# Look-ups of a network's weights on GpSimd in a pinned order, gathered rows added a slot after their fetch, weights' loads behind the squares' exchange

## The chip, the cores and the metric

One core of one Trainium2 chip. The metric is device time of one execution in microseconds (us), the median of several runs; lower is better. Engines are named as in the profile: PE (TensorE), PEld (its weight loads), DVE (VectorE), ACT (ScalarE), POOL (GpSimd), SP (SyncE, which here only issues DMAs). "SPq" and "POOLq" are the instruction streams of SP and POOL that issue DMAs. L953 is line 953 of the kernel before the change.

## The reference

Eight sequences of 512 tokens with 256 channels, float32, pass two layers: a rotating scan with gates, a mixture of 16 experts (2 chosen a token), causal attention, and a gated FFN whose weights are looked up in a table of 16 values.

```python
x = x + _L0_attn_ref(_layernorm(x), ...)       # scan over the tokens, 6 heads
x = x + _L0_ffn_ref(_layernorm(x), ...)        # 16 experts, the best 2 of each token
# _L1_attn_ref: 16 heads of 128, causal, 512 tokens
scores = jnp.einsum('biph,biqh->biqp', k, q)
attn = jax.nn.softmax(masked / jnp.sqrt(jnp.float32(d_head)), axis=-1)
z = jnp.einsum('biqp,biph->biqh', attn, v)
out = jnp.einsum('df,bqf->bqd', W_O, z_flat)
# _L1_ffn_ref: 256 -> 688 -> 256
w = lut[idx]                                   # gate, up and down weights
h = jax.nn.silu(gate) * up
```

The change touches the second layer's attention stage, in which three things run beside the attention itself: the results of the experts are gathered and added to x, the FFN's weights are made from indices and table, and the attention's weights are loaded again for each sequence.

## The kernel before, in words

**Stages.** Layer 0 with its router runs until some 390 us, the experts' blocks to some 530, the attention of layer 1 from there to 2046, and the last FFN to the end at 2277. The attention's loop (L1304 on) goes over 64 pairs of heads (8 sequences of 8 pairs) and in each over its two heads, e = 0 and 1: 128 turns, called slots here. Four slots (two pairs) make a quarter of a sequence's output.

**One slot.** In order: scores of 128-row tiles 0 and 1 of this head (PE `sc`, then DVE `ms` with the row's least value, L1074, then ACT `pr`, the exponential, L1085); the head before ("front") has its probabilities `slots` turned in blocks of 32 by DVE (L1108) and written to the squares in DRAM by four DMAs of SP (L1111); part of the products for the next pair's queries and keys (`nxt`); the head two before ("rear") is weighed: PE `pz` (L1140) from `pT` and `v`, copied by ACT to `zT` (L1147); pending additions of outputs (`in_time`); a gather; a step of the look-ups; the next group's values (`ahead`); scores of tiles 2 and 3; then `exchanged` (L1113), in which SP loads `pT` back from the squares, turned as a whole. There is one `pT` buffer.

**Products of seven.** Queries, keys, values and outputs are made by seven products in place of eight (class Sevens, L230). `first` gives four of them into banks pa and pb, and DVE (sometimes ACT for the copy) makes `p`, `u`, `p` and the first quarter of the result (L249 to L253). `second` gives three more into the same banks, so PE waits for L253 before it goes on with pb, and DVE adds u to it (L262).

**Weights.** `following_weights` (L1001) is called where a weights' tile has been used for the last time; it issues at once two or three loads by SP (L739 to L745), which wait until PE is done with the buffer. Queries' and keys' weights have two buffers each, values' ("v") and outputs' ("o") one. In the first sequence `complete_weights` makes the sums that the products need on POOL (L201 to L205) and writes them to DRAM by a DMA of POOL (L747); later sequences load them.

**Look-ups.** `lookups` (L933) is a generator that does a step each time it is called: in every slot of the sequences 1 to 7, so 112 times. A part of the indices is loaded by ACT's queue (L944); for each of the 16 values DVE compares the indices with it and multiplies by the table's entry (L947, L950), and adds the product to the sum (L953). Four parts of 128 x 688 (`fs`, one value a step) and six of up to 128 x 256 (`fd`, two values a step). Behind the fourth part come four copies (L960) and five sums of fs, one a step.

**Gathers.** `gather` (L890) fetches 128 rows of experts' results by an indirect DMA that POOL issues (L893, buffer `yg`, two of them) and adds them to x by DVE (L900), in the same slot. The rows of sequences 1 to 7 are spread over the first 88 slots: 56 gathers.

**Outputs.** A quarter's `combined` (L1166) makes four differences of 128 x 512 on POOL (`zS`, one buffer), then four pieces of products with the "o" weights follow in later slots, and after a sequence's last quarter `summed` (L1207) makes eight sums on POOL and two pieces of transposes on PE (L1229) read them. `one_out` starts the next piece, at one or two places of a slot.

**What sets the order.** In the loop, the order of PE, DVE and SP is that of the program (manual_schedule, L1287); that of ACT and POOL is made by the scheduler of the language. Each engine runs its own stream in order and waits for semaphores.

Of the kernel before, what the change touches and what calls it, by code (L numbers as in the profile page):

```python
# [10 lines left out]
F32 = mybir.dt.float32  # L11
I32 = mybir.dt.int32
AF = mybir.ActivationFunctionType
ALU = mybir.AluOpType
# [3 lines left out]
P = 128  # L18
NB, T, D = 8, 512, 256
NT = T // P  # L20
# [20 lines left out]
SQ = 32  # L41
# [74 lines left out]
def two_layers(ctx: ExitStack, tc: tile.TileContext, a: dict, out: bass.AP):  # L116
# [79 lines left out]
    def sum_steps(w, eng=nc.vector):  # L196

        a11, a12, a21, a22 = (w[:, n, :] for n in (W_1, W_2, W_3, W_4))
        s1, s2 = w[:, W_5, :], w[:, W_6, :]
        return [  # L200
            lambda: eng.tensor_tensor(s1, a21, a22, ALU.add),  # L201
            lambda: eng.tensor_tensor(s2, s1, a11, ALU.subtract),
            lambda: eng.tensor_tensor(w[:, W_7, :], a11, a21, ALU.subtract),
            lambda: eng.tensor_tensor(a21, a12, s2, ALU.subtract),
            lambda: eng.tensor_scalar(a22, a22, -1.0, None, ALU.mult),  # L205
        ]
# [680 lines left out]
                if s % 12 == 9 and 0 < s // 12 <= 5 or s % 12 == 1 and 1 < s // 12 <= 6:  # L887
                    complete[s % 12 == 1]()

    def gather(b, pool, t, k):  # L890

        y = pool.tile([P, D], F32, name="yg")
        nc.gpsimd.indirect_dma_start(  # L893
            out=y,
            out_offset=None,
            in_=ys,
            in_offset=bass.IndirectOffsetOnAxis(ap=yrow[:, (b * 2 + k) * NT + t : (b * 2 + k) * NT + t + 1], axis=0),
        )
        xt = x_sb[b][:, t, :]
        nc.vector.scalar_tensor_tensor(xt, y, share[:, b, k, t : t + 1], xt, ALU.mult, ALU.add)  # L900

    ygp = ctx.enter_context(tc.tile_pool(name="yg", bufs=2))
    xnp = ctx.enter_context(tc.tile_pool(name="xn", bufs=4))
    with tc.manual_schedule(engines={ENG.PE}):


        first_xn = []
        stats = {}
        for t in range(NT + 1):
            if t < NT:  # L910
                for k in range(2):
                    gather(0, ygp, t, k)
                stats[t] = tile_stats(0, t)
            if t:
                mean, rs = stats[t - 1]
                nc.vector.reciprocal(rs, rs)
                first_xn.append(normed_row(0, xnp, t - 1, mean, rs))
        for b in BEHIND:
            for piece in seqs[b].shared():
                piece()  # L920
# [12 lines left out]
    def lookups(pool):  # L933

        parts = [
            (fs[:, n, :], a[f"idx{w}"][c * P : (c + 1) * P, :], P)
            for n, w, c in ((W_1, 0, 0), (W_2, 0, 1), (W_4, 1, 1), (W_3, 1, 0))
        ]
        behind = []
        parts += [(fd[:k, i, :], a["idx2"][r : r + k, :], k) for i, (r, k) in enumerate(ICH)]  # L940
        for dst, src, k in parts:
            n = src.shape[1]
            idx = pool.tile([P, INTER], I32, tag="idx", name="idx")
            nc.scalar.dma_start(out=idx[:k, :n], in_=src)  # L944
            for v in range(NLUT):
                if v == 0:
                    nc.vector.tensor_scalar(dst, idx[:k, :n], 0.0, lut[:k, 0:1], ALU.is_equal, ALU.mult)  # L947
                else:
                    tmp = pool.tile([P, INTER], F32, tag="tmp", name="tmp")
                    nc.vector.tensor_scalar(  # L950
                        tmp[:k, :n], idx[:k, :n], float(v), lut[:k, v : v + 1], ALU.is_equal, ALU.mult
                    )
                    nc.vector.tensor_add(dst, dst, tmp[:k, :n])  # L953
                if n > T or v % 2:
                    if behind:
                        behind.pop(0)()
                    yield
            if dst is parts[3][0]:
                for n, c, at in ((W_1, 0, APART), (W_2, 1, APART), (W_4, 1, 0), (W_3, 0, 0)):
                    nc.vector.tensor_copy(over[:, c, at : at + OVER], fs[:, n, NF * P :])  # L960
                behind = sum_steps(fs[:, :, : NF * P])


    xtp = ctx.enter_context(tc.tile_pool(name="xt", bufs=2, side="right"))
    with tc.tile_pool(name="big", bufs=2, side="right") as big, tc.tile_pool(
# [31 lines left out]
            return [pool.tile([P, T], F32, tag=tag, name=tag).rearrange("p (k t) -> p k t", k=2) for _ in range(2)]  # L997

        incomplete = []

        def following_weights(n, part):  # L1001
            if part is not None:
                w, complete = load_weights(n, part, part not in seen_parts[n])
                weights[n].append(w)
                seen_parts[n].add(part)
                if complete:
                    incomplete.append((n, complete))
# [49 lines left out]
        class Head:  # L1057
# [29 lines left out]
            def normalized(self, *tiles):  # L1087

                if 0 in tiles:
                    self.slots = ap2.tile([P, NQ, NS, SQ], F32, name="slots")  # L1090
                w = self.slots
                rd = self.rd[:, tiles[0] : tiles[-1] + 1]
                nc.vector.reciprocal(rd, self.den[:, tiles[0] : tiles[-1] + 1])  # L1093
                for i in tiles:

                    for j in range(0, i + 1, 2):
                        n = min(i + 1 - j, 2)
                        at, step = SLOT[j, i], SLOT[j + n - 1, i] - SLOT[j, i]
                        nc.scalar.activation(  # L1099
                            w[:, :, at : at + step + 1 : max(step, 1), :].rearrange("p q j k -> p j q k"),  # L1100
                            self.pr[i][:, j * P : (j + n) * P].rearrange("p (j q k) -> p j q k", q=NQ, k=SQ),
                            AF.Copy,
                            scale=self.rd[:, i : i + 1],
                        )

            def squares_turned(self):

# [27 lines left out]

            def weigh(self):

                pz = pzp.tile([P, T], F32, tag="pz", name="pz")
                for j in range(NT):
                    nc.tensor.matmul(  # L1140
                        pz[:, j * P :].rearrange("p (i q k) -> p i q k", q=NQ, k=SQ),
                        self.v(j),
                        self.of_keys(j),
                        start=(j == 0),
                        stop=(j == NT - 1),
                    )
                nc.scalar.copy(self.z, pz)  # L1147


        late = []  # L1150
# [1 line left out]
        def in_time():  # L1152
            while late:
                late.pop(0)()
# [82 lines left out]
        def outputs(quarter, eng=nc.gpsimd):  # L1237

            quarter.combined(eng)
            last = quarter.q == NGRP - 1  # L1240
            n = quarter.b * NGRP + quarter.q + 1

            def end(*banks):
                quarter.products(3, *banks)
                if n < NB * NGRP:
                    following_weights("o", n % NGRP)
                if last:
                    in_time()
                    quarter.summed(eng)

            pieces = [lambda *banks, i=i: quarter.products(i, *banks) for i in range(3)] + [end]
            if last:
                pieces += [lambda *banks, h=h: quarter.turned(h, *banks) for h in range(2)]
            return pieces

        def one_out():
            if tiles_out:
                tiles_out.pop(0)()
# [1 line left out]
        ALL = NB * NPAIR  # L1260

        together = {1: (1,), 2: (2, 3), 4: (4, 5), 6: (6, 7), NB: (0,)}
        rows_to_gather, since = [], 0
        for c in (1, 2, 4, 6):
            until = (c - 1) * 2 * NPAIR + 2 * NT
            rows = [(b, ygp, t, k) for b in together[c] for t in range(NT) for k in range(2)]
# [17 lines left out]
            pattern=[[-1, P]],  # L1284
            channel_multiplier=1,
        )
        with tc.manual_schedule(engines={ENG.PE, ENG.DVE, ENG.SP}):  # L1287
            seqs[0].xn = first_xn
            for c in range(NC):
                seqs[0].turned(c)  # L1290
            seqs[0].combined()
            following_weights("o", 0)

            pairs[0].first(0)
            pairs[0].first(1, lambda: other_banks(psc, "sc"))
# [3 lines left out]
            groups[0].first(1, lambda: other_banks(ptp, "pt"))  # L1299
            for s in range(2):  # L1300
                groups[0].second(s, s or None)

            front = rear = None
            for p in range(ALL):  # L1304
# [6 lines left out]
                for e in range(2):  # L1311
# [20 lines left out]
                    if rear:  # L1332
                        rear.weigh()
                    in_time()
                    while rows_to_gather and rows_to_gather[0][0] <= 2 * p + e:
                        gather(*rows_to_gather.pop(0)[1])
                    if b:
                        next(look, None)
                    if rear and e and pair % 2 == 0:
                        quarter = Outputs(*divmod(p // 2 - 1, NGRP), done, kept)  # L1340
                        tiles_out += outputs(quarter)
# [11 lines left out]
                    head.scores(3)  # L1353
                    if front and front.by_slots:
                        front.exchanged()
                    in_time()
                    if e and ahead:
                        last_half = p % 2 == 1
                        ahead.second(p % 2, (p // 2 + 2) % NGRP if last_half and p // 2 + 2 < len(groups) else None)
                    if not e and nxt:  # L1360
                        nxt.first(1)
                    if head.by_slots:
# [1 line left out]
                        head.normalized(3)  # L1364

                    complete_weights(*(("v",), (0, 1, "o"))[e])
                    front, rear = head, front

                    if pair == 3 and e == 0 and b + 1 in together:
# [12 lines left out]
                if pair % 2 == 1:  # L1382
                    done = z
            one_out()
            rear.weigh()
            one_out()
            front.turned()
# [208 lines left out]
```

## Time and profile before

| what | us |
|---|---|
| median of 3 runs | 2278.41 |
| lowest and highest run | 2270.70, 2278.88 |
| the profiled execution, its own time | 2278.94 |
| its span, first to last instruction | 2277.2 |
| busy PE, PEld | 2123.3, 1551.5 |
| busy DVE, ACT, POOL | 1716.0, 1181.6, 428.1 |
| DMA: share of 16 engines' time, mean rate | q1 47.5%, q0 3.4%; 160 GB/s |
| granted TensorE clock, mean | 0.989 |

The page gives busy time by engine, the span in 40 slices, the costliest groups of instructions with the idle time of the engine just before them and what ended it. A table of windows gives the same by stretches of time, a list of waits says which engine waited at which instruction for whom (total us, times, longest), a list by form keeps operand shapes apart (count, total us and mean ns of one), and a timeline shows the instructions in order. PE counts as busy to the modelled end of a matmul; idle time of an engine that isn't the bound costs nothing.

### The profile page before, as it was taken

The page shows a single profiled execution, that of the slowest core. Times are in us where ns is not written, and L with a number is a line of the kernel's source. Part 1 is how long each engine was busy: PE and PEld are TensorE (multiplying, and loading weights), DVE is VectorE, ACT ScalarE, POOL GpSimd, SP SyncE. Part 2 cuts the span into 40 slices and gives each one's busy share as a digit, 9 for nine tenths or more (in the row PEclk, how much of TensorE's full clock was granted, in tenths as well). Part 3 has the DMA queues.
Part 4 walks back from the last instruction along what each step waited for, and adds up shares of the span by engine and source line. Part 5 has one row for each costly group of instructions (what it writes and reads, how often), then busy time and mean ns, then how long its engine had stood idle before and what let it go on. Part 6 is the DMA issues. An engine that isn't in the chain of part 4 may idle for free. (4 is left out here: it accounts for less than half of the span.)

```text
span 2277.2 us, 29531 instructions
## 1 busy us (share of the span) xinstructions
PE 2123.3 (93%) x8733; PEld 1551.5 (68%) x8733; DVE 1716.0 (75%) x4269; ACT 1181.6 (52%) x2943; POOL 428.1 (19%) x438
## 2 busy tenths in 40 slices
PE   6999998998899999999999999988999999989999
PEld 3554545886577776777677777766776767658887
DVE  6788887555667778778777877888877887868765
ACT  5767761433565555555556555545555555643211
POOL 0022234002463312121221131121011111010000
PEclk9999999999999999999999999999999999999999
DMA  5111217652677766666757666765666675530000
GB/s 192 46 70 64 75 63 247 193 159 82 191 223 223 221 200 199 211 204 201 226 186 213 205 210 193 215 199 174 185 191 199 190 213 182 176 94 10 19 19 28
DMA packets 208640, 363.98 MB, mean 160 GB/s; under 512 B 27120, under 2 KB 145952, under 8 KB 208480
## 3 DMA queue, kind: packets, MB, share of 16 engines
q1 hardware_dynamic: 197712, 333.62, 47.5%
q0 software_dynamic: 8112, 25.31, 3.4%
q10 hardware_dynamic: 2656, 3.17, 0.4%
q8 instruction: 70, 1.15, 0.2%
q14 instruction: 90, 0.74, 0.1%
HBM read 241.29 MB, written 120.72 MB: 159 GB/s over the span
## 5 line engine op out<-in xcount | busy, mean ns | idle before, releaser
L1099 ACT ACTIVATE slots<-pr,rd 128x128 f32<-128x128 f32 x756 | 302.2, 463 | 236.2 <-DVE rd L1093 162.1
L1140 PE MATMUL pz<-pT,v 128*128 128x512 f32 (+3 forms) x1024 | 306.8, 443 | 30.1 <-DMA pT<-squares 29.7
L1070 PE MATMUL sc<-qk,qk 128*128 128x128 f32 (+3 forms) x1024 | 321.4, 437 | 4.6 <-DVE low L1074 4.5
L1085 ACT ACTIVATE pr<-ms,low 128x128 f32<-128x128 f32 (+3 forms) x512 | 282.0, 552 | 41.1 <-DVE low L1074 39.5
L1140 PEld LDWEIGHTS pz<-pT,v 128*128 128x128 f32 x1024 | 192.0, 192 | 158.7 <-issue 63.9
L1074 DVE CUSTOM_DVE_ANT_0 ms<-sc,mask 128x128 f32<-128x128 f32 (+3 forms) x512 | 235.8, 482 | 50.4 <-PE sc L1070 46.9
L1108 DVE STREAM_TRANSPOSE slots<-slots 128x1280 f32<-128x1280 f32 x126 | 190.2, 1510 | 102.0 <-ACT slots L1099 101.9
L1147 ACT COPY zT<-pz 128x512 f32<-128x512 f32 x128 | 74.9, 585 | 281.9 <-PE pz L1140 260.4
L239 PE MATMUL pb<-tT,w 128*128 128x256 f32 x762 | 208.8, 383 | 3.6 <-DVE qk L253 3.0
L1070 PEld LDWEIGHTS sc<-qk,qk 128*128 128x128 f32 x1024 | 174.9, 193 | 52.0 <-ACT slots L1099 5.3
L893 POOL DMA_INDIRECT yg<-ys,yrow x64 | 66.1, 1032 | 613.2 <-DVE x L900 452.8
L239 PEld LDWEIGHTS pb<-tT,w 128*128 128x128 f32 x762 | 140.2, 192 | 23.1 <-DVE qk L253 5.9
L239 PE MATMUL pa<-xT,w 128*128 128x256 f32 x508 | 151.6, 380 | 0.0
L239 PE MATMUL pb<-wv,tT 128*128 128x256 f32 x378 | 106.5, 390 | 39.9 <-DVE v L253 31.6
L632 POOL DMA_INDIRECT xs<-xn,slot x64 | 83.8, 1309 | 306.1 <-DVE share L642 122.8
L251 DVE TENSOR_TENSOR u<-pa,p 128x256 f32<-128x256 f32 x230 | 96.3, 419 | 50.3 <-ACT p L249 45.3
L239 PEld LDWEIGHTS pb<-wv,tT 128*128 128x128 f32 x378 | 68.2, 189 | 89.8 <-DVE v L253 65.3
L1194 PE MATMUL po<-zS,wo 128*128 128x256 f32 x512 | 125.9, 379 | 1.2 <-DVE kept L1205 1.2
L252 DVE TENSOR_TENSOR p<-pb,u 128x256 f32<-128x256 f32 x230 | 97.5, 424 | 25.1 <-PE pb L239 1.8
L262 DVE TENSOR_TENSOR qk<-pb,u 128x512 f32<-128x512 f32 x127 | 85.1, 670 | 38.0 <-PE pb L239 35.3
L1171 POOL TENSOR_TENSOR zS<-zT 128x512 f32<-128x512 f32 x31 | 40.4, 1302 | 372.8 <-PE po L1194 372.8
L1194 PEld LDWEIGHTS po<-zS,wo 128*128 128x128 f32 x512 | 97.2, 190 | 15.2 <-issue 2.1
(314 smaller groups left out, 4256.7 us busy)
## 6 DMA issues: line engine op xcount, KB each, us to landing
squares<-slots SPq DMA_DIRECT2D x504, 160.0 KB
pT<-squares SPq DMA_DIRECT2D x126, 640.0 KB
w<-sqk SPq DMA_DIRECT2D x112, 320.0 KB
w<-in_aqk SPq DMA_DIRECT2D x144, 128.0 KB
wv<-sv SPq DMA_DIRECT2D x28, 640.0 KB
wo<-so SPq DMA_DIRECT2D x28, 640.0 KB
xb<-xs SPq DMA_DIRECT2D x79, 128.0 KB
ys<-yb SPq DMA_DIRECT2D x79, 128.0 KB
```

The source lines that it names most:

```text
L239: nc.tensor.matmul(to, lhsT, rhs, start=first, stop=True, skip_group_check=True)
L251: nc.vector.tensor_tensor(self.u2, pa[:, 1, :], p1, ALU.add)
L252: nc.vector.tensor_tensor(p1, pb[:, 0, :], self.u2, ALU.add)
L262: nc.vector.tensor_tensor(self.out[:, :2, :], pb, self.u2.unsqueeze(1).to_broadcast([P, 2, HT]), ALU.add)
L632: nc.gpsimd.indirect_dma_start(out=xs, out_offset=bass.IndirectOffsetOnAxis(ap=slot[:, k, t : t + 1], axis=0), in_=self.xn[t], in_offset=None,
L1070: nc.tensor.matmul(sc[:, :kw], self.qT[:, i * P : kw], self.kT[:, :kw], start=True, stop=True)
L1074: nc.vector.tensor_tensor_reduce(out=ms[:, :kw], in0=sc[:, :kw], in1=mask[:, T - kw :], scale=-1.0 / math.sqrt(DH), scalar=3e38, op0=ALU.a ...
L1085: nc.scalar.activation(pr, ms[:, :kw], AF.Exp, bias=low, scale=-1.0, accum_out=self.den[:, i : i + 1])
L1099: nc.scalar.activation(w[:, :, at : at + step + 1 : max(step, 1), :].rearrange("p q j k -> p j q k"), self.pr[i][:, j * P : (j + n) * P].r ...
L1108: nc.vector.transpose(self.slots, self.slots)
L1140: nc.tensor.matmul(pz[:, j * P :].rearrange("p (i q k) -> p i q k", q=NQ, k=SQ), self.v(j), self.of_keys(j), start=(j == 0), stop=(j == NT ...
L1194: nc.tensor.matmul(po[:, m, :], self.w[:, n, k * P : (k + 1) * P], self.sides[n][:, k, :], start=(k == 0), stop=(k == 1),)
```

## The change

1. In `lookups` every operation goes from DVE to POOL: comparisons, additions, the four copies and the five sums. The index loads are issued by POOL's queue in place of ACT's, each at the end of the part before; the first is issued ahead of the loop. The step is called at the end of a slot (behind `complete_weights`) and not behind the gather.
2. POOL joins the engines whose order in the loop is that of the program.
3. `gather` becomes `fetched`, which issues the fetch and hands back the addition; in the loop the addition is made a slot later, at the same place of the slot, ahead of the next fetch.
4. `following_weights` only notes what is to be loaded, but for "o"; `load_following` issues the noted loads, behind `exchanged` and again behind the values' second products.
5. A sequence's last quarter has an empty piece between its products and its transposes.
6. `weigh` writes `pz` with the slots' order of queries (q, i, k), so that PE reads `pT` in long runs; ACT's copy puts them in order.
7. `normalized` names its operands first; its branch for DVE is never taken.

```diff
-    def gather(b, pool, t, k):
+    def fetched(b, pool, t, k):
...
         xt = x_sb[b][:, t, :]
-        nc.vector.scalar_tensor_tensor(xt, y, share[:, b, k, t : t + 1], xt, ALU.mult, ALU.add)
+        return lambda: nc.vector.scalar_tensor_tensor(xt, y, share[:, b, k, t : t + 1], xt, ALU.mult, ALU.add)
...
-        for dst, src, k in parts:
+
+        def indices(dst, src, k):
+            idx = pool.tile([P, INTER], I32, tag="idx", name="idx")
+            nc.gpsimd.dma_start(out=idx[:k, : src.shape[1]], in_=src)
+            return idx
+
+        idx = indices(*parts[0])
+        yield
+        for m, (dst, src, k) in enumerate(parts):
             n = src.shape[1]
-            idx = pool.tile([P, INTER], I32, tag="idx", name="idx")
-            nc.scalar.dma_start(out=idx[:k, :n], in_=src)
             for v in range(NLUT):
                 if v == 0:
-                    nc.vector.tensor_scalar(dst, idx[:k, :n], 0.0, lut[:k, 0:1], ALU.is_equal, ALU.mult)
+                    nc.gpsimd.tensor_scalar(dst, idx[:k, :n], 0.0, lut[:k, 0:1], ALU.is_equal, ALU.mult)
                 else:
                     tmp = pool.tile([P, INTER], F32, tag="tmp", name="tmp")
-                    nc.vector.tensor_scalar(
+                    nc.gpsimd.tensor_scalar(
                         tmp[:k, :n], idx[:k, :n], float(v), lut[:k, v : v + 1], ALU.is_equal, ALU.mult
                     )
-                    nc.vector.tensor_add(dst, dst, tmp[:k, :n])
+                    nc.gpsimd.tensor_add(dst, dst, tmp[:k, :n])
+                if v == NLUT - 1 and m + 1 < len(parts):
+                    following = indices(*parts[m + 1])
...
-                    nc.vector.tensor_copy(over[:, c, at : at + OVER], fs[:, n, NF * P :])
-                behind = sum_steps(fs[:, :, : NF * P])
+                    nc.gpsimd.tensor_copy(over[:, c, at : at + OVER], fs[:, n, NF * P :])
+                behind = sum_steps(fs[:, :, : NF * P], nc.gpsimd)
+            idx = following
...
         def following_weights(n, part):
             if part is not None:
+                to_load.append((n, part))
+                if n == "o":
+                    load_following()
+
+        def load_following():
+            while to_load:
+                n, part = to_load.pop(0)
                 w, complete = load_weights(n, part, part not in seen_parts[n])
...
-                pz = pzp.tile([P, T], F32, tag="pz", name="pz")
+                pz = pzp.tile([P, NQ, NT, SQ], F32, tag="pz", name="pz")
                 for j in range(NT):
                     nc.tensor.matmul(
-                        pz[:, j * P :].rearrange("p (i q k) -> p i q k", q=NQ, k=SQ),
+                        pz[:, :, j:, :].rearrange("p q i k -> p q (i k)"),
                         self.v(j),
-                        self.of_keys(j),
+                        self.pT[:, :, SLOT[j, j] : SLOT[j, j] + NT - j, :].rearrange("p q i k -> p q (i k)"),
...
-                nc.scalar.copy(self.z, pz)
+                nc.scalar.copy(self.z.rearrange("p (i q k) -> p i q k", q=NQ, k=SQ), pz.rearrange("p q i k -> p i q k"))
...
             if last:
-                pieces += [lambda *banks, h=h: quarter.turned(h, *banks) for h in range(2)]
+
+                pieces += [lambda *banks: None] + [lambda *banks, h=h: quarter.turned(h, *banks) for h in range(2)]
...
-        with tc.manual_schedule(engines={ENG.PE, ENG.DVE, ENG.SP}):
+        with tc.manual_schedule(engines={ENG.PE, ENG.DVE, ENG.Pool, ENG.SP}):
...
                     in_time()
+                    while to_add:
+                        to_add.pop(0)()
                     while rows_to_gather and rows_to_gather[0][0] <= 2 * p + e:
-                        gather(*rows_to_gather.pop(0)[1])
-                    if b:
-                        next(look, None)
+                        to_add.append(fetched(*rows_to_gather.pop(0)[1]))
...
                         front.exchanged()
+                    load_following()
                     in_time()
                     if e and ahead:
                         last_half = p % 2 == 1
                         ahead.second(p % 2, (p // 2 + 2) % NGRP if last_half and p // 2 + 2 < len(groups) else None)
+                    load_following()
...
                     complete_weights(*(("v",), (0, 1, "o"))[e])
+                    if b:
+                        next(look, None)
```

`load_following` is also called behind the loads ahead of the loop and once behind the loop.

More of the change, by code (lines that the diff above doesn't have):

```diff
@@ L911, in two_layers @@
                 for k in range(2):
-                    gather(0, ygp, t, k)
+                    fetched(0, ygp, t, k)()
                 stats[t] = tile_stats(0, t)
@@ L999, in two_layers @@
         incomplete = []
+        to_load = []
         def following_weights(n, part):
             if part is not None:
+                to_load.append((n, part))
[4 more added lines that the diff above has]
+                n, part = to_load.pop(0)
                 w, complete = load_weights(n, part, part not in seen_parts[n])
@@ L1098, in normalized @@
                         at, step = SLOT[j, i], SLOT[j + n - 1, i] - SLOT[j, i]
[L1099 to L1104, printed above, removed]
+                        to = w[:, :, at : at + step + 1 : max(step, 1), :].rearrange("p q j k -> p j q k")
+                        pr = self.pr[i][:, j * P : (j + n) * P].rearrange("p (j q k) -> p j q k", q=NQ, k=SQ)
+                        rd = self.rd[:, i : i + 1]
+                        if False:
+                            nc.vector.tensor_scalar(to, pr, rd, None, ALU.mult)
+                        else:
+                            nc.scalar.activation(to, pr, AF.Copy, scale=rd)
             def squares_turned(self):
@@ L1262, in two_layers @@
         together = {1: (1,), 2: (2, 3), 4: (4, 5), 6: (6, 7), NB: (0,)}
-        rows_to_gather, since = [], 0
+        rows_to_gather, to_add, since = [], [], 0
         for c in (1, 2, 4, 6):
@@ L1292, in two_layers @@
             following_weights("o", 0)
+            load_following()
+            next(look)
             pairs[0].first(0)
@@ L1355, in two_layers @@
                         front.exchanged()
+                    load_following()
                     in_time()
@@ L1359, in two_layers @@
                         ahead.second(p % 2, (p // 2 + 2) % NGRP if last_half and p // 2 + 2 < len(groups) else None)
+                    load_following()
                     if not e and nxt:
@@ L1384, in two_layers @@
             one_out()
+            load_following()
             rear.weigh()
```

## The prediction

> **What bounds the kernel now.** I read the page first (PE 93% busy, DVE 75%, ACT 52%, POOL 19%), then the table of windows, cut where each of layer 1's eight sequences starts, to see in which stage PE stands idle.
>
> ```profile
> 600.00:776.00 176.00, 166.03 (x694) 124.35 (x693) 125.73 (x337) 102.39 (x290) 80.09 (x110) 1.00 0.73 220
> 776.00:960.00 184.00, 173.67 (x721) 130.15 (x720) 146.18 (x366) 102.10 (x290) 40.90 (x36) 0.99 0.68 209
> ...
> 1505.00:1693.00 188.00, 173.99 (x721) 131.62 (x720) 153.40 (x391) 102.05 (x289) 28.36 (x25) 0.98 0.63 190
> ...
> 2046.00:2277.00 231.00, 225.96 (x1045) 191.48 (x1043) 158.16 (x353) 52.23 (x112) 0.00 (x0) 1.00 0.06 19
> ```
>
> After the length, the columns are PE, PEld, DVE, ACT and POOL busy, granted clock, DMA share. In the attention (600 to 2046) PE is busy 1354.8 of 1446 us, so it bounds that stage and at most 91 us can go. The FFN behind it leaves PE 5 us idle, and the change touches nothing before 530. The first sequence has no look-ups and takes 176 us; the next six take 179 to 188. So I asked who ends PE's waits in 600 to 2046:
>
> ```profile
> PE pb L239 <- DVE v L253: 31.6, 19, 3.6
> PE pz L1140 <- DMA pT<-squares: 27.0, 32, 2.3
> PE po L1229 <- POOL kept L1210: 10.3, 7, 2.7
> PE pb L239 <- DVE qk L262: 8.1, 11, 1.4
> PE sc L1070 <- DVE low L1074: 4.5, 1, 4.5
> PE po L1194 <- DMA wo<-in_ao: 4.3, 5, 1.8
> ```
>
> These six (total us, times, longest) are 85.8 of 90.2 us. The timeline at the longest waits of the first row shows why DVE is late:
>
> ```profile
> 1539.94 0.67 DVE L1233 TENSOR_TENSOR x<-x,po 128x512 f32<-128x512 f32 x1
> ...
> 1540.91 1.46 DVE L953 TENSOR_TENSOR fd<-fd,tmp 128x256 f32<-128x256 f32 x1
> ...
> 1543.68 1.37 DVE L953 TENSOR_TENSOR fd<-fd,tmp 128x256 f32<-128x256 f32 x1
> ...
> 1546.42 0.70 PE L239 MATMUL pb<-wv,tT 128*128 128x256 f32 x2 [3.14 <-DVE v L253]
> ```
>
> The four look-up instructions of that slot stand in DVE's fixed order ahead of the additions that PE needs, and hold it from 1540.5 to 1545.0. The first sequence's waits have no such row.
>
> **Part 1, look-ups off DVE.** L947 to L960 take 2.3 + 2.1 + 76.7 + 58.0 + 54.2 + 0.5 = 194 us of DVE, plus five sums of fs (L201 to L205, 5.3 us), in 112 slots: 1.8 us a slot. DVE leaves PE waiting only where it is late, so I count the waits: of the 31.6 us I take 28 (bounds 15 and 31.6), of the 4.5 (at 2008, behind two look-ups and the token sides) 3 (0 to 4.5), of the 8.1 only 2 (0 to 8.1), as the first sequence has 1.5 us of it without look-ups. **-33**.
>
> POOL gets them. It has shown no such operation; the nearest rows are these:
>
> ```profile
> L1173 POOL TENSOR_TENSOR zS<-zT 128x512 f32<-128x512 f32 x31 | 41.8, 1350 | 0.0
> L205 POOL TENSOR_SCALAR w<-w 128x128 f32<-128x128 f32 x12 | 6.9, 573 | 0.0
> L205 POOL TENSOR_SCALAR wo<-wo 128x256 f32<-128x256 f32 x4 | 3.6, 892 | 0.0
> L204 POOL TENSOR_TENSOR wo<-wo 128x256 f32<-128x256 f32 x4 | 2.9, 725 | 0.0
> ```
>
> Additions: 0.735 us at 256 columns, 0.46 at 128, so 2.18 ns a column and 1.68 us at 688. Multiplications: 0.875 at 256 (wo and wv), 0.573 at 128, so 2.36 ns a column, 1.89 us at 688. On DVE the look-up (569 and 344 ns) stands 1.1 and 1.24 times as long as L205 does (486 at 640 columns, 278 at 256); with that ratio 2.1 and 1.08 us. Sum: 64 x 2.1 + 60 x 1.68 + 96 x 1.08 + 90 x 0.735 = 405 us, and 16 for the sums, copies and ten index loads (0.62 us each, from L747). A slot is 183.5 / 16 = 11.5 us. POOL's own work in four slots is four zS (5.5), fetches (56 x 1.03 / 112 x 4 = 2.1) and a quarter of eight sums (1.6): 9.2 of 46 us. So 9.2 us a slot are free for steps of 3.8 (688 wide) or 3.6 us. Cost on the path: 0 while a step stays under 9.2.
>
> POOL's order is now pinned. Behind a look-up stand the next fetch, the four zS, the sums and the weights' sums. A look-up waits for nothing but its index load, issued a slot ahead, so POOL runs it early and is back before zT (PE, ACT) ends the zS's wait. The fetch waits for the yg buffer that the addition of the slot before frees. In the first sequence (no look-ups) weights' sums queue behind fetches: +2 (0 to 8).
>
> **The lock.** L953 at 256 columns takes 425 ns by its median and 1.46 and 1.37 us at 1540 and 1543, beside POOL's zS; L1108's 126 transposes average 1510 with a longest of 1514. [...]
>
> **Part 2, additions a slot later.** DVE waited 6.9 us in all for yg, none of it in a row of PE's waits; 0. The same 0.47 us stands at the same place of DVE's order.
>
> **Part 3, loads behind the exchange.** SP waits 141 us for PE's pa to free a weights' buffer (L739) ahead of the pT load. Before the 2.3 us wait at 1407.5, SP issued wo and w loads (1344 KB) from 1397.9 to 1400.3, then pT at 1400.4, which landed 7 us later; at the 200 GB/s of the page's row a w pair (448 KB) ahead is 2.2 us, and the mean wait is 0.8. But 61 pT loads wait for their own squares anyway, and wo's loads are still issued at once. Of 27.0 I take **-20** (-5 to -27). The pair's loads are two pairs ahead of use and v's stay where they were: 0.
>
> **Part 4, an empty piece before the transposes.** PE waits 10.3 us for the eight sums (6.3 us on POOL). Half a slot more covers them unless a look-up is ahead; POOL has that done. **-9** (-5 to -10.3).
>
> **Part 5, pz in another order.** PE takes 592 ns for pz and for sc at 512 columns, though pz reads runs of 32; writing such runs: 0 (0 to 5). ACT's permuted copy (585 ns, 128 times) has ACT's 48% idle as cover: 0 (0 to 8).
>
> **The clock.** Each of seven stretches of 10 us around 797, 1408, 1498, 1592, 1640, 1735 and 2008 shows a clock of 0.83, and each has a wait of 2.2 us or more: 3.4 us at half rate, 1.7 lost. Six of seven go: **-10** (-3 to -12). [...]
>
> **Sum.** -33 - 20 - 9 - 10 = -72; +2, +5, and +7 for the next late thing (ACT's chain pr, slots, transpose, squares, which with less PE idle has a shorter slot): -58. From 2278.9 (the profiled execution; span 2277.2) 2221, and as the median is 2278.4, **2220**. Check: the first sequence without look-ups runs 7.5 us faster than the next six do; 7 x 7.5 = 52, of which part 4 is some, and part 3 comes on top.
>
> **Rivals.**
> - *POOL becomes the bound (slower).* If the look-up on POOL takes over 10.5 ns a column (9.2 - 1.68 = 7.5 us at 688), the slot is POOL's: fetches and zS come late and DVE and PE wait. At 12 ns a step is 10.2 us, 64 slots x 1.0 = +64, with 26 saved elsewhere: 2317. For: int32 in, a compare and a multiply, no row on POOL. Against: L205's 2.36 ns, 4.5 times less. [...] 7%.
> - *The lock eats it.* [...] 13%.
> - *The change doesn't order what it says, or PE takes up new waits of the same size* (squares behind the late loads): within 11 us of 2278. 8%.
> - *Nearly all idle goes*: -33 - 9 - 27 - 10 - 12 = 2188. 10%.
> - The forecast, 2205 to 2245: 62%.
>
> Faster by over 0.5% (11 us, about what this measurement can tell from no change): 0.85; within: 0.07; slower: 0.08. Range 2188 to 2260: from the best case to the lock's.
>
> **What would show it.** DVE busy in 776 to 2046 falls by some 140 us or more; the row "PE pb <- DVE v" falls under 5 us; pT's row under 10; "po L1229 <- POOL kept" is gone; POOL's look-ups at 688 last about 2.1 us; sequences take 175 us; the clock's pieces go. Wrong it is if the look-ups take over 5 us, if DVE's x L900 grows to 2 us, or if POOL's zS are what PE waits for.

## The result and the profile after

The changed kernel takes 2253.2 us (median of 4 runs, 2247.6 to 2257.9) against 2278.4 before; the ratio is 0.9896 with a 95% interval of 0.9865 to 0.9927. Faster, as forecast, but by 25 us and not by 58. The profiled execution took 2247.6 us (span 2245.8), the fastest of the four, and stands 31 us below the profiled one of before.

The windows of the profile after, cut again where each sequence starts (columns as in the prediction: length, PE, PEld, DVE, ACT and POOL busy, granted clock, DMA share, GB/s):

```profile
598.00:774.00 176.00, 166.93 (x696) 125.24 (x696) 125.19 (x332) 102.56 (x290) 86.48 (x113) 1.00 0.71 222
774.00:956.00 182.00, 172.53 (x719) 129.45 (x718) 125.01 (x335) 102.49 (x289) 110.32 (x71) 0.99 0.67 210
...
1490.00:1672.00 182.00, 172.24 (x722) 130.28 (x721) 121.07 (x326) 102.64 (x289) 95.85 (x97) 0.99 0.64 201
...
2014.00:2245.80 231.80, 226.45 (x1047) 191.90 (x1045) 158.25 (x353) 52.23 (x112) 0.00 (x0) 1.00 0.06 19
```

DVE is relieved (146 to 125 us in the second sequence, 153 to 121 in the sixth), POOL has taken the work (41 to 110, 28 to 96), the FFN is as it was. But the sequences still take 178 to 182 us, not 175. PE's waits in 598 to 2014 (total us, times, longest) tell why:

```profile
PE pz L1159 <- DMA pT<-squares: 39.9, 33, 3.3
PE po L1213 <- DMA wo<-in_ao: 17.3, 20, 3.4
PE pb L239 <- DVE qk L262: 8.1, 11, 1.1
PE pb L239 <- DVE qk L253: 2.5, 7, 0.4
```

The rows for DVE's v (31.6 us before) and POOL's kept (10.3) are gone. pT's row has risen from 27.0 to 39.9 and wo's from 4.3 to 17.3. Of 42 us taken away, 26 came back under two other names.

POOL's look-ups, by form:

```profile
L956 POOL TENSOR_SCALAR tmp<-idx,lut 128x688 f32<-128x688 int32 x60 | 156.0, 2600 | 4.6
L959 POOL TENSOR_TENSOR fs<-fs,tmp 128x688 f32<-128x688 f32 x60 | 98.7, 1646 | 5.0
L956 POOL TENSOR_SCALAR tmp<-idx,lut 128x256 f32<-128x256 int32 x75 | 86.4, 1152 | 6.5
L959 POOL TENSOR_TENSOR fd<-fd,tmp 128x256 f32<-128x256 f32 x75 | 54.6, 728 | 6.3
```

A step is 2.60 + 1.65 = 4.25 us at 688 columns and 3.76 at 256 (two values): less than half of the 9.2 us that a slot had free.

### The profile page after: what moved, and what is told of

It reads as the page before. It is cut to its first block, busy times and chain, and to the rows that moved or that the text cites. A ratio compares the mean times of both kernels' runs of the same rounds, so it can differ in the third digit from the quotient of the medians.

```text
span 2245.8 us, 29655 instructions
## 1 busy us (share of the span) xinstructions
PE 2108.6 (94%) x8733; PEld 1546.5 (69%) x8733; DVE 1539.8 (69%) x3950; ACT 1184.2 (53%) x2943; POOL 868.7 (39%) x767
## 3 DMA queue, kind: packets, MB, share of 16 engines
q8 instruction: 70, 1.15, 0.2%
## 4 chain that ended last, share of the span: by engine, by line
PE 67%; DMA 15%; DVE 12%; ACT 3%; issue 3%; SPq 1%; POOL 0%; DVEq 0%; POOLq 0%; ACTq 0%
PE pb L239 14%; PE pz L1159 11%; PE pa L239 10%; PE sc L1088 9%; DMA pT<-squares 9%; PE po L1213 6%; PE py L1482 4%; PE pgu L841 3%; DMA scale<-dscale 2%; PE pyb L859 2%; DMA squares<-slots 1%; DVE slots L1127 1%; DVE v L379 1%; PE pa L432 1%; DMA wo<-in_ao 1%
## 5 line engine op out<-in xcount | busy, mean ns | idle before, releaser
L956 POOL TENSOR_SCALAR tmp<-idx,lut 128x256 f32<-128x256 int32 (+2 forms) x150 | 259.5, 1730 | 12.5
L1127 DVE STREAM_TRANSPOSE slots<-slots 128x1280 f32<-128x1280 f32 x126 | 190.2, 1510 | 103.3 <-ACT slots L1123 102.3
L1213 PE MATMUL po<-zT,wo 128*128 128x256 f32 x384 | 97.0, 390 | 17.3 <-DMA wo<-in_ao 17.3
```

The lines of the kernel that those rows point to most:

```text
L956: nc.gpsimd.tensor_scalar(tmp[:k, :n], idx[:k, :n], float(v), lut[:k, v : v + 1], ALU.is_equal, ALU.mult)
L1127: nc.vector.transpose(self.slots, self.slots)
L1213: nc.tensor.matmul(po[:, m, :], self.w[:, n, k * P : (k + 1) * P], self.sides[n][:, k, :], start=(k == 0), stop=(k == 1),)
```

## The experiments

Theory A: the waits stood one behind the other in the same slots. A wait taken away lets PE come earlier to the next thing, and that is then the late one. Theory B is the prediction's: each row is a term of its own. Rivals C (late loads do harm) and D (POOL's work costs) stand beside them. Ratios are to the kernel before, with 95% intervals.

**What relieving DVE is worth alone.** `e11`: no look-up on any engine. The weights' tiles are set to zero once on POOL ahead of the loop; nothing else is changed. The lines:

```diff
-                    if b:
-                        next(look, None)
```

> The kernel before without any look-up on any engine (the FFN's weights are left at zero, so its result is left out of the output). It gives what the relief of DVE is worth when nothing is put on POOL. Theory A (pT's exchange and wo stand right behind DVE's lateness): the row of DVE's v goes, pT's and wo's rise by 15 us or more together; ratio 0.988 to 0.996. Theory B (the prediction's part 1 with its share of the clock): 0.980 to 0.984.

Measured: 0.9948 (0.9930 to 0.9966), 12 us. PE's waits in 596 to 2040:

```profile
PE pz L1141 <- DMA pT<-squares: 54.8, 49, 2.9
PE po L1195 <- DMA wo<-in_ao: 16.9, 14, 3.7
PE po L1230 <- POOL kept L1211: 8.8, 7, 2.3
```

DVE's v row is gone, and pT has doubled, wo quadrupled: 35 us of the rows for v and low went, 40 came. One slot shows how. In the kernel before (first fence) PE waits 2.20 us for DVE's v and comes to pz at 1599.11; in `e11` (second) it comes earlier and waits 2.31 us for pT, until 1599.10:

```profile
1591.92 0.84 PE L239 MATMUL pb<-wv,tT 128*128 128x256 f32 x2 [2.20 <-DVE v L253]
...
1599.11 2.32 PE L1140 MATMUL pz<-pT,v 128*128 128x512 f32 x8
```

```profile
1593.07 1.99 PE L1195 MATMUL po<-zT,wo 128*128 128x256 f32 x8 [0.57 <-DMA wo<-in_ao]
...
1599.10 2.42 PE L1141 MATMUL pz<-pT,v 128*128 128x512 f32 x8 [2.31 <-DMA pT<-squares]
```

Counted slot by slot: in the 18 slots in which PE waited over 0.3 us for v or low before (35.5 us in all), its waits for pT and wo rise from 2.8 to 29.7 us. So 27 of the 40 us stand in the very slots that were relieved, as Theory A has it; the other 13 are spread over other slots, and their cause is not shown. Of the 10 us between the two spans, at most 5 are the clock: the stretches in which the granted clock falls to 0.50 add up to 27 us in 600 to 2046 before (eight of 3.4 us) and to 17 in `e11`; from the clock of 0.50 I estimate that such a stretch costs at most half its length. The rest of the gain is not traced.

`e5`: look-ups on POOL, POOL's order pinned. `e10`: the same with the additions a slot later.

In both the look-ups are changed as shown under "The change"; the lines that pin POOL's order and, in `e10` alone, those that make the addition later:

```diff
-        with tc.manual_schedule(engines={ENG.PE, ENG.DVE, ENG.SP}):
+        with tc.manual_schedule(engines={ENG.PE, ENG.DVE, ENG.Pool, ENG.SP}):
...
+                    while to_add:
+                        to_add.pop(0)()
```

> The kernel before with the look-ups on POOL and POOL's order pinned, and nothing else (loads, gathers, pieces and pz as before). Theory A (what DVE's lateness hid comes up behind it): the row of PE for DVE's v is gone, wo's row goes from 4 to some 14 and pT's from 27 to 45 to 58, the kept row is small (POOL's sums no longer wait for DVE's look-ups); ratio to before 0.990 to 0.997, so 7 to 23 us of the 33 us of the prediction's part 1 plus its share of the clock. Theory B (each wait a term of its own): ratio 0.982.

> The kernel before with the look-ups on POOL, POOL's order pinned, and the additions a slot after their fetch; loads, pieces and pz as before. Theory A (with the look-ups alone DVE waited 102 us for fetches, and PE 20.6 us for DVE's qk): DVE's wait for yg falls under 5 us, PE's row for qk to some 8, pT's row stays over 45; ratio 0.993 to 0.999. Prediction's step (the later addition is worth nothing): 1.002 to 1.005, as with the look-ups alone.

Measured: e5 1.0036 (1.0018 to 1.0053), slower than before; e10 0.9924 (0.9899 to 0.9950). In e5 the waits of DVE for fetched rows (first fence) and of PE (second) in 596 to 2030 are:

```profile
DVE x L900 <- DMA yg<-ys,yrow: 102.4, 29, 10.3
```

```profile
PE pz L1149 <- DMA pT<-squares: 52.6, 47, 3.0
PE pb L239 <- DVE qk L262: 20.6, 18, 6.0
PE po L1203 <- DMA wo<-in_ao: 13.0, 17, 3.0
```

With POOL in program order the fetch is issued behind POOL's other work (the sums of weights from 686 to 689 where the wait is longest), and an addition in the same slot holds DVE up to 10.3 us. A slot later that wait is gone, the qk row is 5.7, and pT's row stays at 51.0. Both ratios lie outside what Theory A had said: e5 well above its 0.990 to 0.997, e10 just below its 0.993 to 0.999.

**POOL's load.** `e3`: the changed kernel without the look-ups; the weights' tiles are set to zero as in `e11`.

> The changed kernel without any look-up (the FFN's weights are left at zero, so its result is left out of the output; its products still run). Rival D (the look-ups on POOL cost, by the lock on DVE's additions or by late fetches, zS and sums): faster by 8 us or more than the changed kernel. Theory A: POOL's work is hidden wholly; PE's rows for pT and wo stay within 5 us, time 2253 within 5.

Measured: 0.9925 (0.9899 to 0.9952), with pT 47.0 and wo 15.6: not faster than the changed kernel (0.9896, and 0.9886 in `e7` below). Rival D falls; the look-ups on POOL are hidden. That pT's row rises by 7 us without them, more than the 5 expected, is not explained.

**The loads.** `e6`: the loads behind the exchange, alone on the kernel before. `e2`: the changed kernel with every load at once.

```diff
             if part is not None:
                 to_load.append((n, part))
-                if n == "o":
-                    load_following()
+                load_following()
```

> The kernel before with the loads behind the exchange and nothing else. Theory A: pT's row falls by 5 to 12 us from 27, DVE's v row stays over 25 us and wo's under 6; ratio 0.993 to 0.999. Theory B (the prediction's part 3, -20): 0.991. Rival C (late loads harm pT): over 1.000 with pT's row over 30.

> The changed kernel with every weights' load issued where it was issued before. Theory A: the late loads are not what makes pT and wo late; the wo row stays at some 15 us, pT's row stays at 40 or rises by up to 10, time 2253 to 2263. Rival C (loads behind the exchange run into the next squares and into wo, and SP waits 282 us for squares at its exchange): both rows fall to what they were before (27 and 4), 2225 to 2235.

Measured: e6 0.9988 (0.9971 to 1.0004), pT from 27 to 19.2 and DVE's v from 31.6 to 37.2; e2 0.9963 (0.9940 to 0.9985), with pT at 58.5. Rival C falls: late loads help pT, by more than Theory A had allowed in e2 (58.5 us where it had said 50 at most). Alone they gain some 3 us, which the interval can't tell from nothing: pT's row gives 7.8 us and DVE's v takes 5.6. Where DVE is relieved they gain 15 to 20 (e2 against the changed kernel, e10 against e1 below).

**The empty piece.** `e1` and `e15`: the changed kernel without it; `e7` and `e16`: the changed kernel again. `e13`: the piece alone on the kernel before. `e14`: before with only POOL's order pinned and the additions later.

```diff
-                pieces += [lambda *banks: None] + [lambda *banks, h=h: quarter.turned(h, *banks) for h in range(2)]
+                pieces += [lambda *banks, h=h: quarter.turned(h, *banks) for h in range(2)]
```

> The changed kernel without the empty piece ahead of the transposes. Theory A (waits stood one behind the other, and the taken one uncovered the next): PE's wait for POOL's kept sums comes back with some 10 us, and the 3 us waits for pT at the start of each sequence (797, 979, 1156 ...: some 20 of the 39.9 us of that row) shrink by as much; the time stays at 2253 within 5. Theory B (the prediction's: each wait is a term of its own): the kept row's 10 us come on top, pT's row keeps its 40 us, 2263.

> The changed kernel once more, to stand on the same chip beside the others. All theories: ratio 0.987 to 0.993, as measured; PE's rows pT some 40 and wo some 17 us.

Measured: e1 0.9837 (0.9811 to 0.9863), e7 0.9886 (0.9864 to 0.9907): without the piece it was faster, which neither theory had, and the kept row did not come back (1.2 us). So four more:

> The changed kernel without the empty piece, once more and beside the changed kernel: ratio 0.981 to 0.986 if the piece costs some 0.5%; equal to the changed kernel's within 0.2% if the first comparison was chance.

> The changed kernel on the same chip as the one without the piece: ratio 0.987 to 0.991.

> The kernel before with the empty piece ahead of the transposes, and nothing else. If the piece takes away only what stands in front of the next pT wait: the kept row goes (10 us to under 2), pT's row rises from 27 by 5 to 15 us, ratio 0.998 to 1.004. The prediction's part 4 (-9): 0.996.

> The kernel before with POOL's order pinned and the additions a slot after their fetch; the look-ups stay on DVE, no empty piece. If PE waited for the kept sums because the scheduler put the next quarter's first zS ahead of the eighth sum, the kept row goes to under 3 us without the piece; DVE's v row stays over 25 us; ratio 0.995 to 1.000. If it was the length of the eight sums, the kept row stays at some 10.

Measured, on one chip: e15 0.9838 (0.9810 to 0.9866) and e16 0.9884 (0.9853 to 0.9914), 2242 against 2252 us; e13 1.0066 (1.0042 to 1.0090); e14 1.0066 (1.0045 to 1.0088). PE's waits in e13 (two lines), then in e14:

```profile
PE pz L1140 <- DMA pT<-squares: 39.4, 31, 3.2
PE pb L239 <- DVE v L253: 36.4, 21, 3.6
```

```profile
PE pb L239 <- DVE v L253: 40.0, 21, 3.1
PE pz L1140 <- DMA pT<-squares: 40.0, 44, 2.6
...
PE po L1229 <- POOL kept L1210: 2.9, 4, 0.7
```

The piece alone removes the kept row (10.3 us); pT's row rises by 12 us and v's by 5, and the kernel is 0.7% slower, more than expected. The 12 us stand in the seven slots in which PE had waited for kept: it waits 4.4 us for pT in these slots before and 16.5 with the piece. The pinned order takes 7.4 of the 10.3 us of the kept row without any piece, so most of that wait was not the length of the eight sums. POOL's timeline before shows what it was:

```profile
971.89 5.98 POOL L1210 TENSOR_TENSOR kept<-kept 128x256 f32<-128x256 f32 x7 [12.71 <-DVE kept L1205]
977.83 1.27 POOL L1171 TENSOR_TENSOR zS<-zT 128x512 f32<-128x512 f32 x1
979.06 0.72 POOL L1210 TENSOR_TENSOR kept<-kept 128x256 f32<-128x256 f32 x1
```

The scheduler had put the next quarter's first zS (1.27 us) ahead of the eighth sum, at all seven places; the pinned order has the eight in a row. Still, e14 is 0.7% slower than the kernel before, where 0.995 to 1.000 was expected: pT's row rises by 13 us and v's by 8, and why is not shown. Where the piece takes the transposes out of the slot, PE stands at pz sooner. The changed kernel's timeline at the same place:

```profile
969.12 0.71 SPq L739 DMA_DIRECT2D w<-in_aqk  x1
969.87 0.65 SPq L743 DMA_DIRECT2D w<-sqk  x1
970.98 0.33 SPq L739 DMA_DIRECT2D wo<-in_ao  x1
971.36 0.43 SPq L743 DMA_DIRECT2D wo<-so  x1
971.96 0.32 SPq L1135 DMA_DIRECT2D pT<-squares  x1
...
979.40 1.13 PE L1159 MATMUL pz<-pT,v 128*128 128x512 f32 x2 [3.05 <-DMA pT<-squares]
```

1344 KB of weights are in front of pT, since "o" is loaded at once and takes the noted pair with it; pT is there 7.4 us after its issue. Such a wait, of 2.2 to 3.3 us, stands at the start of each sequence (797, 979, 1156, 1335, 1514, 1695, 1873). Behind three of the seven (797, 1335, 1514) the granted clock falls to 0.50 for 3.4 us; a window of the changed kernel:

```profile
790.00:805.00 15.00, 12.06 (x46) 8.26 (x45) 7.77 (x21) 6.80 (x21) 12.88 (x10) 0.89 0.83 279
```

In windows of 1 us the granted clock is 0.50 from 797 to 800. 0.89 over 15 us is 3.4 us at half rate: by the same estimate at most 1.7 us more.

**The weights of the outputs.** wo's wait has its own place. Before (first fence) and after (second), in the same slot:

```profile
1083.98 0.71 SPq L739 DMA_DIRECT2D wo<-in_ao  x1
...
1086.97 0.70 PE L239 MATMUL pb<-wv,tT 128*128 128x256 f32 x2 [1.67 <-DVE v L253]
...
1089.02 1.24 PE L1194 MATMUL po<-zT,wo 128*128 128x256 f32 x5
```

```profile
1079.84 0.70 SPq L739 DMA_DIRECT2D wo<-in_ao  x1
...
1080.98 0.59 PE L239 MATMUL pb<-wv,tT 128*128 128x256 f32 x2
...
1084.23 1.13 PE L1213 MATMUL po<-zT,wo 128*128 128x256 f32 x4 [1.13 <-DMA wo<-in_ao]
```

From the load's issue to its use PE had 5.0 us before, of which it waited 1.67 for DVE; without that wait it is there in 3.3 and waits 1.13 for wo. Two versions test this. `e9`: the "o" loads of a sequence's first quarter behind the exchange. `e4` (and `e12`, the same again): W_1 and W_2, which the first piece uses, in a tile of their own, loaded again right after that piece; the other five behind the last piece; both behind the exchange. `e8`: e4 without the empty piece.

```diff
-                if n == "o":
+                if n == "o" and part:
                     load_following()
```

```diff
-                if n == "o":
-                    load_following()
...
+            two = wtp.tile([P, 2, f], F32, tag="wo", name="wo", bufs=1)
+            nc.sync.dma_start(out=two, in_=a["ao"][part, :, : 2 * f].rearrange("p (k f) -> p k f", k=2))
...
+        rest = w.rest = wtp.tile([P, 5, f], F32, tag="wrest", name="wrest", bufs=1)
...
+            def begin(*banks):
+                quarter.products(0, *banks)
+                if n < NB * NGRP:
+                    following_weights("o", n % NGRP)
```

> The changed kernel in which the outputs' weights of a sequence's first quarter, noted at the last piece of the sequence before, are loaded behind the exchange too (those of the other quarters at once, as in the changed kernel). Theory A: in that slot 1344 KB stood in front of pT, so the 3 us waits at the start of each sequence (some 20 of the 40 us in pT's row) go and wo's row stays at some 17; ratio 0.978 to 0.984, 15 to 25 us below the changed kernel. Rival C: pT's row stays over 35 and the time within 5 us of the changed kernel.

> The changed kernel with the outputs' weights in two tiles: W_1 and W_2 are loaded again right after the first piece of a quarter, three or four slots ahead of their use, the other five behind the last piece, and both behind the exchange. Theory A (wo needs only 11 us from load to use and pT has 1344 KB in front of it in the slot of a sequence's last piece): the wo row falls from 17 to under 4 us, pT's row from 40 to some 20, the time to 2225 within 8. Rival C: the wo row goes, pT's stays at 40: 2238.

> The kernel with the outputs' weights in two tiles once more, to stand beside the one without the piece on the same chip: ratio 0.964 to 0.969.

> The changed kernel with the outputs' weights in two tiles, and without the empty piece ahead of the transposes. POOL's sums have been in time without that piece (1.2 us of waits for them in the kernel without it), so Theory A: the same as with the piece, ratio 0.964 to 0.969; if the piece costs by itself (the kernel without it was measured 0.6% below the changed one), 0.960 to 0.964.

Measured: e9 0.9812 (0.9793 to 0.9832), 17 us below e7 on the same chip. pT's row shows 38.8 in e7 and 36.7 in e9, but 4.5 of the 36.7 are the first pz of the stage, at 596.2, which waits 4.6 us in e7 too and there starts at 593.8, ahead of the window. Like for like the row falls from 38.8 to 32.3 us, where Theory A had said by some 20. At the seven starts of sequences the waits fall from 22.3 to 14.4 us. The clock does more: in 600 to 2030 there are 30.6 us at half rate in e7 (six stretches, three of them of 6.8 us) and 3.4 in e9, so at most 13.6 us by the same estimate. With the shorter waits that is enough for the 15 us between the two spans. e4 0.9666 (0.9640 to 0.9691), e12 0.9647 (0.9621 to 0.9673), e8 0.9665 (0.9640 to 0.9689). PE's waits in e12, 596 to 2030:

```profile
PE pz L1186 <- DMA pT<-squares: 18.8, 16, 3.8
PE pb L239 <- DVE qk L262: 8.6, 11, 1.4
PE pb L239 <- DVE qk L253: 4.2, 14, 0.6
PE pb L239 <- DVE v L253: 1.5, 1, 1.5
```

wo is gone, pT is below what it was before the change: 2201 us, 78 below before and some 50 below the changed kernel, the best version here. Theory A had the rows right and the time 25 us too high (2225). Of the 50 us, 37 are the two rows (pT and wo, 55.7 us in e16 and 18.8 in e12), and at most 10 the clock (27 us at half rate in e16, 7 in e12). There the piece no longer matters (e8 and e12 overlap).

## Why the prediction was wrong, point by point

**Part 1, the sum.** The rows were right: v, low and qk together fell by 35 us (33 forecast). The step that failed is the term "+7 for the next late thing". It looked at ACT's chain and the slot in general, not at each place for what stands right behind the wait. There stood pT and wo, only just in time: in e11 their rows rose by 40 us, 27 of them in the very slots that were relieved. Parts 1 and 2 with their share of the clock, the lock and the rest were to give -29 (-33, -10, +2, +5, +7); e10 measures -17.

**POOL and the lock.** Look-ups of 2.60 and 1.15 us for 2.1 and 1.08, 441 us in all for 405: the ratio taken from DVE was too small at 688 columns, and the limit of 9.2 us a slot held. The lock, DVE's instructions taking longer beside POOL's as L953 does at 1540: no run shows the +5 that stands for it in the sum. x L900 rose from 492 to 561 ns, xnt from 420 to 495, L218 from 1360 (seven of its eight beside a zS, at 1492 to 1498) to 1497 (all eight), 8 us of DVE in all; no row of PE's shows it, and e3, without look-ups, is not faster (0.9925 against 0.9896). ms at 512 columns (690 ns before, 691 after) and the transposes (1510 in both) took no longer. The lock's end of the range, 2260, did not come.

**The pinned order**, +2 (0 to 8): with the later additions alone it costs 15 us (e14), in pT's and v's rows. Where DVE is relieved no such cost shows: e10, pinned and with the look-ups on POOL, has 0.9924, e11 without look-ups and with the free order 0.9948. Why the two differ stays open.

**Part 2** was put at 0 since DVE hardly waited for yg. That was so because POOL's free order fetched ahead: before the change POOL's fetches wait 453 us for DVE to free a buffer. Under the pinned order the later addition is worth 25 us (e5 against e10). I had looked at the wait in the old order only.

**Part 3**, -20: 3 us alone, 20 on top of parts 1 and 2 (e10 0.9924 to e1 0.9837; part 5 lies in it). The mechanism held: the loads ahead of pT make it late. That the size fits is luck in part. pT's row was to go from 27 to 7; it goes from 51.0 (e10) to 37.0 (e1), since it had more to give once DVE was on time, and the changed kernel still has 39.9 where "under 10" was the sign.

**Part 4**, -9: the wrong sign. It measures +10 (e16 against e15), and +15 alone (e13). The step that PE waits for the length of the eight sums (6.3 us) failed: 7.4 of the 10.3 us came from the order on POOL, which the pinning mends, and the piece takes work from in front of pT. In e16 PE's waits are 6 us longer than in e15, 3 of them for pT at the starts of sequences; the rest of the 10 us is not traced.

**Part 5**, 0: pz at 512 columns takes 622 ns in the mean (623 before; 592 is the mean of sc), and ACT's copy still 586 by its median.

**The clock**, -10: from eight half-rate stretches of 3.4 us in the attention to four in the profiled execution, by estimate some 7 us. That execution is the fastest of its kernel; in another, near the median (e16), there are seven, one of them of twice the length, so nothing was gained. Those behind the long DVE waits went, and others came behind pT's.

So -17 (1 and 2), -20 (3) and +10 (4) make -27 beside the 25 measured. Of the 33 us missed, 19 are part 4's sign and 12 what part 1 uncovered. The check by the first sequence, 7.5 us faster without look-ups (7 x 7.5 = 52), misled: without look-ups in any sequence e11 gains 12 us. That the first sequence is faster because it has no sequence's end before it is likely, but no run shows it.

## What to carry to other kernels

A list of waits is not a list of gains: for each wait, go to the same place in the timeline and see by how much the next operand would be late if that wait were gone. When an engine's order is pinned, look again at every wait that the free order had hidden. A load that is waited for right behind its issue is mended best by an earlier issue (a tile split by the time of last use): here that was worth 50 us, moving the load behind the exchange (e9) 17.

## What the runs showed of the hardware that was not expected

- A look-up of 48 x 256 on POOL takes as long as one of 128 x 256 (1140 and 1152 ns), and two operations on int32 cost 3.35 ns a column (from 1152 and 2600 ns) where L205's single one on float32 costs 2.36 (from 573 ns at 128 columns and 875 at 256, before).
- In these two executions the length of a wait of PE does not decide alone whether 3.4 us at half rate follow. In the kernel before they follow one of 2.20 us at 1592 and not one of 3.14 at 1546; in the changed kernel one of 2.94 at 797 and not one of 3.17 at 1873. From 500 us to the end of the attention the stretches at a granted clock of 0.50 last 3.4 us (ten before, four after) or 6.8 (one after, at 591.8).
- Shortening waits may have been worth more by the clock than by the wait in e9: pT's row fell by 6.5 us, and 27 us at half rate went, by estimate at most 13.6 us.
